# A graph attention layer on one Trainium2 core: batches of eight tiles, with Q and E laid out by feature

## The chip, the cores and the metric

The kernel runs on one core of a Trainium2 chip. Its time is the device time of one execution in microseconds (us). Engines are called TensorE (PE; PEld is its weight load), VectorE (DVE), ScalarE (ACT), GpSimd (POOL) and SyncE (SP); "ACTq", "SPq" and so on are the sequencers that feed them. SBUF is the on-chip memory, PSUM the memory that TensorE writes.

## What is computed

There are N = 6250 nodes with 128 features and E = 206,250 edges, sorted by destination, each with 128 features. With eight heads of sixteen features:

```python
Qh = (h @ WQ).reshape(N, H, D); Kh = (h @ WK).reshape(N, H, D); Vh = (h @ WV).reshape(N, H, D)
Eh = (edge_attr @ WE).reshape(-1, H, D)
score = jnp.einsum('ehd,ehd,ehd->eh', Kh[src], Qh[dst], Eh) * inv_sqrt_d
score = jnp.exp(jnp.clip(score, -5.0, 5.0))
msg = Vh[src] * score[:, :, None]
wV = jax.ops.segment_sum(msg, dst, num_segments=N)
Z = jax.ops.segment_sum(score, dst, num_segments=N)
h_out = wV / (Z[:, :, None] + 1e-06)
x = _layernorm(x + h_out)
```

## The kernel before

**Tiles and batches.** The edges are cut into 1612 tiles of 128; `cut_batches` (L62) makes batches of B = 4 tiles, the last eight tiles in smaller ones. At the start K and V of all nodes go as rows of 1 KB into a table `kv` in memory (`table`, L256), while the first twelve batches gather rows of x and project them themselves (`project`, L408).

**K and V of an edge.** For each tile `gather` (L388) issues one indirect DMA from GpSimd (L397), which brings the 128 rows of K and V of the tile's source nodes. The first gather of a batch waits by hand (L401 to L405) for TensorE's expansion `qps` of a batch some way back: `lag` (L343) is 12 batches at first and falls by one every 40 batches to 3. The other gathers of the batch wait for nothing else that is written out. Buffers: GB = 14 batches.

**Column tiles.** Some tiles, one at the end of two batches in five from batch 32 on, are not gathered (L392). Their 128 columns of x are copied one by one out of the transposed x, which stays in SBUF, with four bytes per partition and an address from a register: 96 on ScalarE in 12 runs of 8, 32 on VectorE in 4 runs of 8 (`columns`, L352; COLA, COLV). Each run is preceded by one load of its addresses into registers (L365, on the sequencer), the copies are L370. TensorE then projects the tile (`project_columns`, L379), VectorE puts it in place (L386). 146 tiles are built so.

**Q of an edge.** Q's rows of a window of 42 nodes are held in three bfloat16 parts (126 rows, `qw`). A one-hot of the destinations, turned so that edges are on the free axis (`onehotT`, `stage_0t`, L450), expands them: in `stage_a` each tile's 128 columns of `onehotT` are the weights and `qw` is streamed (L464). E's product takes each tile's edge features as weights and streams `we` (L469). Both results have edges on partitions.

**Scores and messages.** `stage_b` on VectorE: K times Q (L475), times E (L478), sum per head (L481), clip (L484). `weigh` on ScalarE: the exponent into PSUM (L490) and into the message tile (L492). `messages` on VectorE: V times the exponent (L519). `stage_c` on TensorE: a one-hot of destinations within a window of 64 (`stage_0`, L437, two batches in one operation) times the messages, summed in PSUM over eight tiles (L541); ScalarE copies two such sums at once (L552). `finish` (L507) puts windows together, `layernorm` (L735) follows step by step through `fill`.

**Order of the work.** From batch 12 on the order of instructions on every engine is the order in which the program writes them. The loop (L585) writes for step b: loads on SP, expansion and E product of batch b, gathers of batch b+2, the first half of ScalarE's column copies, the score steps of batch b−1 with one-hots of batch b+2 and small steps between them, the messages of batch b−2, VectorE's column copies, the exponents of batch b−1, ScalarE's other half of columns, and the sums of batch b−2.

Of the kernel before, what the change touches and what calls it, by code (L numbers as in the profile page):

```python
# [20 lines left out]
B = 4  # L21
# [8 lines left out]
GB = 14  # L30
XB = 12
LOCK = XB + 6
STEP = 3
GLEAD = 2
OHB = 5
# [5 lines left out]
AHEAD = 2  # L41
EB = 6
SLAG = 2
# [8 lines left out]
COL0 = 32  # L52
COLP = (5, 2)
COLA = (8, 12)
COLV = (8, 4)
COLL = 8
RING = 4096
SUMS = 8
# [4 lines left out]
def cut_batches():  # L63
    out, t = [], 0
    while t < NT:
        k = B
        if t >= NT - TAIL:
            k = 2 if NT - t > 3 else 1
        out.append(range(t, t + k))
        t += k  # L70
    return out
# [30 lines left out]
def edge_attention(ctx: ExitStack, tc: tile.TileContext, x, xT, srcT, srcC, dstT, dstB, dst0, bnd, lo, eaT,  # L102
# [26 lines left out]
    onehots = [cp.tile([P, HW + 2 * B * P], F32, name=f"onehot{i}") for i in range(OHB)]  # L129
# [11 lines left out]
    with ExitStack() as fast:  # L141
# [80 lines left out]
        def count_inside():  # L222
# [7 lines left out]
            pc = psT.tile([1, 1], F32, name="pc", tag="oT")  # L230
# [9 lines left out]
        psT = fast.enter_context(tc.tile_pool(name="psT", bufs=2, space=bass.MemoryType.PSUM))  # L240
        psA = fast.enter_context(tc.tile_pool(name="psA", bufs=2, space=bass.MemoryType.PSUM))
        psX = fast.enter_context(tc.tile_pool(name="psX", bufs=1, space=bass.MemoryType.PSUM))

        iota_p = psX.tile([P, HW], F32, name="iota_p")
        exp_p = psX.tile([P, B, H], F32, name="exp_p")
        nc.vector.tensor_copy(iota_p, iota_f[:, :HW])

        def pair_bank(i, name, shape):

            pool, tag = ((psE, "eps"), (psT, "oT"), (psQ, "qps"), (psT, "oT"))[i % 4]  # L250
            return pool.tile(shape, F32, name=name, tag=tag)
# [32 lines left out]
        def q_rows(q):  # L284
            n = min(P, N - q * P)
            ps = psT.tile([P, D], F32, name="qrows", tag="oT")
# [56 lines left out]
        def lag(b):  # L343

            return max(STEP, 12 - (b - LOCK) // 40)

        col_tiles, xT_bytes = {}, xT_sb.bitcast(U8)
        used = [0]
# [23 lines left out]
        def project_columns(b):  # L372

            if b not in col_batches:
                return
            g = gathered[b]
            k = col_batches.index(b)
            pk = psT.tile([P, 2 * D], F32, name="colkv", tag="oT")
            nc.tensor.matmul(pk, col_tiles.pop(k), wkv_sb, start=True, stop=True)  # L379
            projected.append((g, pk))  # L380
# [27 lines left out]
        def project(g, n):  # L408

            pt = psT.tile([P, B, P], F32, name="xtps", tag="oT")  # L410
            for i in range(n):
                nc.tensor.transpose(pt[:, i, :], g[:, i, :D], ident)
            xgT = wp.tile([P, B, P], F32, name="xgT", tag="kq", bufs=2)
            nc.scalar.copy(xgT[:, :n], pt[:, :n])
            for i in range(0, n, 2):
                k = min(2, n - i)
                pk = pair_bank(i // 2, "kvps", [P, 2, 2 * D])
                for j in range(k):
                    nc.tensor.matmul(pk[:, j, :], xgT[:, i + j, :], wkv_sb, start=True, stop=True)  # L419
                nc.scalar.copy(g[:, i:i + k, :], pk[:, :k, :])  # L420

        def together(b):

            t0 = batches[b][0]
            n = len(batches[b])
            if n == B and b + 1 < nbat and len(batches[b + 1]) == B and t0 % (2 * B) == 0:
                return [b, b + 1]
            return [] if n == B and t0 % (2 * B) else [b]

        def stage_0(b):  # L430
            group = together(b)
            if not group:
                return
            t0, n = batches[b][0], sum(len(batches[i]) for i in group)
            tl = onehots[used[0] % OHB]
            used[0] += 1
# [3 lines left out]
            for i in group:  # L440
                st8[i] = tl, HW + (batches[i][0] - t0) * P - HW * pair_of(batches[i][0])[1], None

        def stage_0t(b):
            group = together(b)
            if not group:
                return
            t0, n = batches[b][0], sum(len(batches[i]) for i in group)
            ohT = wp.tile([QROWS, 2 * B * P], BF16, name="onehotT", bufs=3)
# [3 lines left out]
            for i in group:  # L452
                tl, at, _ = st8[i]
                k = (batches[i][0] - t0) * P
                st8[i] = (tl, at), ohT[:, k:k + len(batches[i]) * P]

        def stage_a(b, g):
            t0, n = batches[b][0], len(batches[b])
            if b < XB:
                project(g, n)  # L460
            oh, ohT = st8.pop(b)
            pq = psQ.tile([P, B, D], F32, name="qps")
            for i in range(n):
                expanded[b] = nc.tensor.matmul(pq[:, i, :], ohT[:, i * P:i * P + P], loaded[t0 // WT],  # L464
                                               start=True, stop=True)
            pe = psE.tile([P, B, D], F32, name="eps")
            ea = ea_tiles(t0, n)
            for i in range(n):
                nc.tensor.matmul(pe[:, i, :], ea[:, i * P:i * P + P], we_sb, start=True, stop=True)  # L469
            st8[b] = [n, g, oh, pq, pe]  # L470

        def stage_b(b):
            n, g, oh, pq, pe = st8[b]
            t0 = wp.tile([P, B, D], F32, name="kq", bufs=2)
            nc.vector.tensor_tensor(t0[:, :n], g[:, :n, :D], pq[:, :n], op=ALU.mult)  # L475
            yield
            t1 = wp.tile([P, B, D], F32, name="kqe", bufs=2)
            nc.vector.tensor_tensor(t1[:, :n], t0[:, :n], pe[:, :n], op=ALU.mult)  # L478
            yield
            sc = wp.tile([P, B, H], F32, name="sc")  # L480
            nc.vector.tensor_reduce(sc[:, :n], t1[:, :n].rearrange("p b (h d) -> p b h d", h=H),  # L481
# [3 lines left out]
            st8[b] = [n, g, oh, sc]  # L485

        def weigh(b):
# [3 lines left out]
            m = wp.tile([P, B, MW], F32, name="msg")  # L491
# [8 lines left out]
        def add_windows(ps, q, first, stop):  # L500

            parts = windows(q)
            for i, (k, s) in enumerate(parts):
                nc.tensor.matmul(ps, shift[:, P - s:2 * P - s], sums[k // 2][:, k % 2],  # L504
                                 start=first and i == 0, stop=stop and i == len(parts) - 1)

        def finish(j):  # L507

            q = 2 * j
            ps = psT.tile([P, 2, MW], F32, name="finps", tag="oT")  # L510
# [13 lines left out]
        def stage_c(b):  # L524
            n, g, oh, m = st8.pop(b)
            for i in range(n):
# [7 lines left out]
                u = k if final else k // 2  # L534
                first = u not in aggs
                if first:
                    aggs[u] = psA.tile([P, 2, MW], F32, name="agg")
                    if final:
                        add_windows(aggs[u][:, 0], QL, True, False)
                tail = k == NT if t == NT - 1 else pair_of(t + 1)[0] != k  # L540
                nc.tensor.matmul(aggs[u][:, 0 if final else k % 2], oh[0][:, oh[1] + i * P:oh[1] + i * P + P], m[:, i, :],  # L541
                                 start=not final and t % (2 * G) == 0, stop=tail)
                if tail and final:
# [5 lines left out]
                    norms.append(layernorm(nc, sp, aggs.pop(u)[:, :1], xbs.pop(QL), out, QL, 1, stores))  # L549
                elif tail and (k % 2 == 1 or t == LAST - 1):  # L550
                    sums[u] = sp.tile([P, 2, MW], F32, name="sum", bufs=SUMS)
                    nc.scalar.copy(sums[u][:, :k % 2 + 1], aggs.pop(u)[:, :k % 2 + 1])  # L552
                    while len(finished) < QL // 2 and all(v // 2 <= u for v, _ in windows(2 * len(finished) + 1)):
                        ready.append(len(finished))
                        finished.append(u)

        gathered = {b: gather(b) for b in range(2)}
        for b0 in range(0, NB, KB):
# [3 lines left out]
            for b in range(len(gathered), min(XB, nbat)):  # L562
                if (b - 2 if b < 5 else b) * KB > b0:
# [249 lines left out]
```

## Time and profile before

| | |
|---|---|
| median of 3 runs | 2586.32 us (2565.03 to 2592.5) |
| profiled execution | 2567.26 us |
| its span, first to last instruction | 2565.4 us |
| mean granted TensorE clock | 0.75 |
| DMA | 380.81 MB, mean 148 GB/s |
| gathers on GpSimd | 1418 of K and V rows, 48 of x |
| ScalarE column copies | 14016, 189 ns each from start to end |

A row of a group reads: line, engine, operation, output<-input, shapes, count, then busy us and mean ns of one, then the idle time before them and what ended it. A row of stretches reads: stretch in us from the start, its length, busy us and count of each engine asked for, granted clock, DMA share, GB/s. "issue" is time in which an engine waited for nothing that the profile shows. The copies of one run overlap: each lasts 0.19 us from start to end, and they start less than 0.1 us apart.

### The profile page before, as it was taken

Reading aid. Unit: us, or ns where it says so; the run is one execution under the profiler, and the core shown is the slowest. Engines: PE = TensorE matmul, PEld = TensorE weight load, DVE = VectorE, ACT = ScalarE, POOL = GpSimd, SP = SyncE. Lnnn points to the kernel's source line nnn. Section 1 sums busy time; section 2 is a strip of 40 time slices with the busy share of each in tenths; the row PEclk is TensorE's granted clock in tenths of the full one; section 3 lists DMA queues with packets and bytes.
Section 4 is the critical chain, followed back from the end, with each engine's and each line's share of the span. In section 5 each row is a group of like instructions: output and inputs, shape, how many; then the busy total and the mean of one; then the engine's idle time right before and its main releaser. Section 6 shows DMA issues by size and latency. Waiting matters only on the chain.

```text
span 2565.4 us, 49832 instructions
## 1 busy us (share of the span) xinstructions
PE 1624.0 (63%) x9342; PEld 1407.1 (55%) x9342; DVE 1843.5 (72%) x8070; ACT 1644.0 (64%) x15015; POOL 1396.9 (54%) x1473
## 2 busy tenths in 40 slices
PE   5656566676666666666666655667666656566665
PEld 3446555565665555555555555556556555455555
DVE  2436678878777777777767777877877777777786
ACT  1211667777776677676767767777776666776760
POOL 6446555555555455555554555555655555555564
PEclk7777777777776777776777768777876777777787
DMA  7545445645554464455444544564654455545542
GB/s 233 153 130 179 136 125 157 176 134 169 153 148 132 134 176 138 123 147 174 130 135 136 175 140 129 147 175 137 183 147 126 136 144 164 145 131 144 173 145 79
DMA packets 171028, 380.81 MB, mean 148 GB/s; under 512 B 58653, under 2 KB 84569, under 8 KB 170707
## 3 DMA queue, kind: packets, MB, share of 16 engines
q0 software_dynamic: 69584, 189.03, 25.8%
q1 hardware_dynamic: 99983, 187.46, 24.4%
q14 instruction: 244, 2.00, 0.2%
q8 instruction: 77, 1.26, 0.2%
q10 hardware_dynamic: 1140, 1.06, 0.1%
HBM read 362.61 MB, written 14.81 MB: 147 GB/s over the span
## 4 chain that ended last, share of the span: by engine, by line
ACT 46%; issue 25%; DVE 11%; PE 8%; ACTq 6%; another core or an unknown queue 3%; DMA 1%; DVEq 0%; SPq 0%
ACT xcol L370 42%; ACTq L365 6%; DVE xcol L370 2%; PE agg L541 2%; PE eps L469 2%; ACT msg L492 2%; DVE kqe L478 2%; DVE msg L519 1%; DVE kq L475 1%; PE finps L504 1%; ACT exp_p L490 1%; PE kvps L419 1%; DVE sc L481 1%; ACT sum L552 1%
## 5 line engine op out<-in xcount | busy, mean ns | idle before, releaser
L397 POOL DMA_INDIRECT kvrows<-kv,src x1418 | 1350.3, 952 | 1120.4 <-PE qps L464 420.4
L370 ACT COPY xcol<-xT_sb 128x4 uint8 x14016 | 1499.0, 189 | 573.0 <-issue 560.3
L541 PE MATMUL agg<-msg,onehot 128*128 128x136 f32 x3224 | 639.1, 358 | 441.3 <-DVE msg L519 316.8
L541 PEld LDWEIGHTS agg<-msg,onehot 128*128 128x128 f32 x3224 | 562.4, 254 | 492.2 <-ACT msg L492 276.5
L469 PE MATMUL eps<-we_sb,ea 128*128 128x128 f32 x3224 | 599.6, 343 | 164.5 <-DVE kqe L478 95.3
L469 PEld LDWEIGHTS eps<-we_sb,ea 128*128 128x128 f32 x3224 | 517.8, 244 | 220.6 <-DVE kqe L478 128.7
L519 DVE TENSOR_TENSOR msg<-kvrows,exp_p 128x512 f32<-128x512 f32 x406 | 275.9, 679 | 488.8 <-ACT exp_p L490 276.4
L370 DVE COPY xcol<-xT_sb 128x4 uint8 x4672 | 410.9, 192 | 30.2 <-issue 23.0
L464 PE MATMUL qps<-qw,onehotT 126*128 126x128 bf16 x1612 | 193.5, 254 | 240.7 <-DVE kq L475 163.2
L464 PEld LDWEIGHTS <-onehotT 126*128 126x128 bf16 x1612 | 154.7, 117 | 325.3 <-issue 306.8
L478 DVE TENSOR_TENSOR kqe<-kq,eps 128x512 f32<-128x512 f32 x406 | 274.6, 676 | 52.3 <-remote 30.7
L475 DVE TENSOR_TENSOR kq<-kvrows,qps 128x512 f32<-128x512 f32 x406 | 273.7, 674 | 37.5 <-remote 21.3
L481 DVE TENSOR_REDUCE sc<-kqe 128x32 f32<-128x512 f32 x406 | 272.8, 672 | 5.8 <-DVE y L761 0.5
L490 ACT ACTIVATE exp_p<-sc 128x32 f32<-128x32 f32 x406 | 78.3, 193 | 139.7 <-DVE sc L484 76.8
L437 DVE TENSOR_TENSOR onehot<-iota_p,dst_sb 128x512 f32<-128x512 f32 (+2 forms) x206 | 137.6, 669 | 11.0 <-remote 9.0
L379 PE MATMUL colkv<-wkv_sb,xcol 128*128 128x256 f32 x292 | 127.9, 533 | 0.0
L504 PE MATMUL finps<-sum,shift 128*128 128x136 f32 x640 | 95.2, 310 | 17.1 <-ACT sum L552 11.1
L504 PEld LDWEIGHTS finps<-sum,shift 128*128 128x128 f32 x640 | 91.1, 219 | 19.6 <-ACT sum L552 13.1
L492 ACT ACTIVATE msg<-sc 128x32 f32<-128x32 f32 x406 | 87.2, 215 | 22.2 <-issue 21.7
L450 DVE TENSOR_SCALAR onehotT<-relb,node 126x1024 bf16<-126x1024 bf16 (+2 forms) x206 | 99.8, 485 | 1.8 <-DMA relb<-relD 1.7
L484 DVE TENSOR_SCALAR sc<-sc 128x32 f32<-128x32 f32 x406 | 83.7, 206 | 4.2 <-issue 3.8
L379 PEld LDWEIGHTS colkv<-wkv_sb,xcol 128*128 128x128 f32 x292 | 69.1, 285 | 0.0
(73 smaller groups left out, 568.9 us busy)
## 6 DMA issues: line engine op xcount, KB each, us to landing
ea<-eaT SPq DMA_DIRECT2D x201, 512.0 KB
relb<-relD SPq DMA_DIRECT2D x100, 504.0 KB
kvrows<-kv,src POOLq DMA_INDIRECT x1418
qw<-qs SPq DMA_DIRECT2D x202, 31.5 KB
kv<-kvst SPq DMA_DIRECT2D x12, 512.0 KB
qs<-qst SPq DMA_DIRECT2D x48, 96.0 KB
xb<-x SPq DMA_DIRECT2D x24, 128.0 KB
out<-h SPq DMA_DIRECT2D x24, 128.0 KB
```

The costliest lines, as they stand in the source:

```text
L365: at = nc.values_load_multi_w_load_instructions(col_at[k % col_half:k % col_half + 1, k // col_half, j:j + size], engines=(engine,), min_v ...
L370: copy(to[:, 4 * (j + c):4 * (j + c) + 4], xT_bytes[:, ds(at[c] - XT_AT, 4)])
L379: nc.tensor.matmul(pk, col_tiles.pop(k), wkv_sb, start=True, stop=True)
L397: ins = nc.gpsimd.indirect_dma_start(out=g[:k, i, :f], out_offset=None, in_=rows, in_offset=bass.IndirectOffsetOnAxis(ap=src_col(t)[:k], a ...
L464: expanded[b] = nc.tensor.matmul(pq[:, i, :], ohT[:, i * P:i * P + P], loaded[t0 // WT], start=True, stop=True)
L469: nc.tensor.matmul(pe[:, i, :], ea[:, i * P:i * P + P], we_sb, start=True, stop=True)
L475: nc.vector.tensor_tensor(t0[:, :n], g[:, :n, :D], pq[:, :n], op=ALU.mult)
L478: nc.vector.tensor_tensor(t1[:, :n], t0[:, :n], pe[:, :n], op=ALU.mult)
L481: nc.vector.tensor_reduce(sc[:, :n], t1[:, :n].rearrange("p b (h d) -> p b h d", h=H), axis=AX.X, op=ALU.add)
L504: nc.tensor.matmul(ps, shift[:, P - s:2 * P - s], sums[k // 2][:, k % 2], start=first and i == 0, stop=stop and i == len(parts) - 1)
L519: nc.vector.tensor_tensor(m[:, :n, :D].rearrange("p b (h d) -> p b h d", h=H), g[:, :n, D:].rearrange("p b (h d) -> p b h d", h=H), exp_p[ ...
L541: nc.tensor.matmul(aggs[u][:, 0 if final else k % 2], oh[0][:, oh[1] + i * P:oh[1] + i * P + P], m[:, i, :], start=not final and t % (2 * ...
```

## The change

A batch is eight tiles (B = 8), and one iteration of the loop handles eight. E and Q are made with features on partitions: `qw` and `we` are the weights, and 512 edges at a time are streamed. ScalarE copies Q out of PSUM into `eq`, VectorE multiplies it in place by E's product (`product`), TensorE turns the result with eight transposes into PSUM (`turn`), and VectorE multiplies that by K. The score has one multiplication by K (1024 elements wide) and one with E per eight tiles. The expansion of batch b+1 is written in iteration b, after the transposes of batch b. PSUM holds Q, E and the turned product in two banks each, one buffer each; sums, exponents and the small users share the last two banks.

Constants go with it: GB 8, XB 6, one batch of gathers written ahead, a lag of 6 batches that falls by one every 20 to 2. ScalarE's part of a column tile is 6 runs of 16 copies (COLA), and three batches in four have a column tile. The built program has 12,960 column copies on ScalarE, which is 135 tiles (the description says 133), with 810 loads. Window sums are copied one by one.

```diff
-B = 4
+B = 8
-GB = 14
-XB = 12
-LOCK = XB + 6
-STEP = 3
-GLEAD = 2
-OHB = 5
+GB = 8
+XB = 6
+LOCK = XB + 3
+STEP = 2
+GLEAD = 1
+OHB = 3
-EB = 6
-SLAG = 2
+EB = 5
+SLAG = 1
-COL0 = 32
-COLP = (5, 2)
-COLA = (8, 12)
+COL0 = 16
+COLP = (4, 3)
+COLA = (16, 6)
 COLV = (8, 4)
-COLL = 8
+COLL = 4
...
-            return max(STEP, 12 - (b - LOCK) // 40)
+            return max(STEP, 6 - (b - LOCK) // 20)
...
+            pq = psQ.tile([P, B * P], F32, name="qps")
+            pe = psE.tile([P, B * P], F32, name="eps")
+            for i in range(0, n * P, G * P):
+                j = min(n * P, i + G * P)
+                expanded[b] = nc.tensor.matmul(pq[:, i:j], loaded[t0 // WT], ohT[:, i:j], start=True, stop=True)
+            for i in range(0, n * P, G * P):
+                j = min(n * P, i + G * P)
+                nc.tensor.matmul(pe[:, i:j], we_sb, ea[:, i:j], start=True, stop=True)
+            qT = wp.tile([P, B * P], F32, name="eq", bufs=2)
+            nc.scalar.copy(qT[:, :n * P], pq[:, :n * P])
+            st8[b] = [n, qT, pe]
+
+        def product(b):
+            n, qT, pe = st8[b]
+            nc.vector.tensor_tensor(qT[:, :n * P], qT[:, :n * P], pe[:, :n * P], op=ALU.mult)
+            st8[b] = [n, qT]
+
+        def turn(b):
+            n, eq = st8[b]
+            pp = psP.tile([P, B, D], F32, name="pps")
             for i in range(n):
+                nc.tensor.transpose(pp[:, i, :], eq[:, i * P:i * P + P], ident)
+            st8[b] = [n, pp]
+
+        def stage_b(b, g):
+            n, pp = st8[b]
+            t0 = wp.tile([P, B, D], F32, name="kq", bufs=1)
+            nc.vector.tensor_tensor(t0[:, :n], g[:, :n, :D], pp[:, :n], op=ALU.mult)
             yield
...
+            steps = stage_b(b - 1, gathered.pop(b - 1)) if 0 <= b - 1 < nbat else iter(())
+            next(steps, None)
+            if b < nbat:
+                product(b)
+            fill()
+            if b + 1 < nbat:
+                turned_one_hots(b + 1)
+            fill()
+            if b < nbat:
+                turn(b)
+            if b + 1 < nbat:
+                stage_a(b + 1)
+            next(steps, None)
+            fill()
+            if 0 <= b - 2 < nbat:
+                messages(b - 2)
+            fill()
+            next(steps, None)
+            if 0 <= b - 1 < nbat:
+                weigh(b - 1)
+                one_hots(b - 1)
```

The gathers of batch b+1 and the first half of ScalarE's columns are written at the head of iteration b; after the lines above come the small users, VectorE's columns, ScalarE's other half, and the sums of batch b−2.

191 lines of the change are left out of this document (71 added, 120 removed).

## The prediction

> **What bounds the kernel now.** I read, in this order, the page's busy shares and chain of waits, the totals of waits, the register loads' line, and then stretches of ScalarE's column copies cut by where GpSimd's gathers stood.
>
> ```profile
> span 2565.4 us, 49832 instructions
> PE 1624.0 (63%) x9342; PEld 1407.1 (55%) x9342; DVE 1843.5 (72%) x8070; ACT 1644.0 (64%) x15015; POOL 1396.9 (54%) x1473
> ACT 46%; issue 25%; DVE 11%; PE 8%; ACTq 6%; another core or an unknown queue 3%; DMA 1%; DVEq 0%; SPq 0%
> ACT xcol L370 <- issue: 560.3, 1033, 1.2
> DVE msg L519 <- ACT exp_p L490: 276.4, 151, 6.1
> ACT exp_p L490 <- DVE sc L484: 76.8, 22, 18.7
> L365 ACTq TENSOR_LOAD <-col_at x1752: 535/555/1799, 251.8 to 2489.9; - x195
> L312 SPq TENSOR_LOAD <-starts x13: 686/1158/1179, 83.5 to 2395.8; - x13
> 252.00:2490.00 2238.00, 1681.01 (x7680) 0.75 0.51 148
> 252.00:2490.00 2238.00, 1594.13 (x14844) 0.75 0.51 148
> ```
>
> No engine is busy over 72%, but the chain is ScalarE: 46% its work, 25% "issue", 6% its sequencer's loads. The largest wait is ScalarE's column copies behind "issue", 560 us in 1033 gaps: no semaphore was missing, the next copy simply did not start. VectorE waits 276 us for ScalarE's exponents, ScalarE only 77 us for VectorE's scores. The last two rows are VectorE and ScalarE in the stretch in which columns are copied. The loads' row gives that stretch: 251.8 to 2489.9 us, 2238.1 us. The schedule starts columns in batch 25 and ends them in batch 389, so 365 batches of four tiles, 6.13 us each, **12.26 us per eight tiles**; there are 182.5 such units. ScalarE's busy time is 8.7 us of each (1594.13 / 182.5), the gaps 3.1 us (560.3 / 182.5): together 11.8 of 12.26. ScalarE is the bound there.
>
> When do the gaps come? First GpSimd in a run of seven gathers, then the column copies on ScalarE in the seven slots of 1.25 us from its start, and in one slot after it (columns: length, busy us and count, clock, DMA share, GB/s).
>
> ```profile
> 1209.04 0.94 POOL L397 DMA_INDIRECT kvrows<-kv,src  x1 [1.36 <-PE qps L464]
> 1210.29 0.94 POOL L397 DMA_INDIRECT kvrows<-kv,src  x1 [0.30 <-issue]
> ...
> 1209.04:1210.29 1.25, 1.25 (x15) 1.00 1.05 346
> 1210.29:1211.54 1.25, 1.09 (x12) 1.00 1.05 368
> 1211.54:1212.79 1.25, 0.38 (x3) 1.00 1.06 377
> 1212.79:1214.04 1.25, 0.37 (x3) 1.00 1.08 243
> 1214.04:1215.29 1.25, 0.11 (x1) 0.65 1.01 222
> 1215.29:1216.54 1.25, 0.29 (x2) 0.50 1.02 259
> 1216.54:1217.79 1.25, 0.46 (x3) 0.50 0.95 300
> 1219.00:1220.25 1.25, 1.07 (x11) 0.50 0.37 133
> ```
>
> Beside the first two gathers ScalarE copies at full rate, from the third on it falls to one to three copies a slot, and after the run it recovers. The DMA engines are full from the first slot on, so their load alone is not it. The next rows are sums over all 155 runs of back-to-back gathers between 300 and 1500 us: copies beside the first gather, the second, the third, the fourth (105 runs have one), and everything past 5 us.
>
> ```profile
> sum 193.75, ACT 179.15; mean ACT 1.16
> sum 193.75, ACT 175.93; mean ACT 1.14
> sum 193.54, ACT 129.71; mean ACT 0.84
> sum 130.04, ACT 45.15; mean ACT 0.43
> sum 139.63, ACT 38.71; mean ACT 1.11
> ```
>
> Busy shares 92%, 91%, 67%, 35%, 28%. A lone copy counts 0.19 us and one in a row 0.095 us (below), so I read 11.6, 11.4, 7, 3 and 2.5 copies per 1.25 us. **A long unbroken run of gathers starves ScalarE; a short one does not.** That is what the change touches without naming it.
>
> **The change part by part**, per eight tiles of the column stretch.
>
> ```profile
> 1220.19 2.38 ACT L370 COPY xcol<-xT_sb 128x4 uint8 x24
> 1222.47 0.19 ACT L490 ACTIVATE exp_p<-sc 128x32 f32<-128x32 f32 x1
> 1222.61 0.22 ACT L492 ACTIVATE msg<-sc 128x32 f32<-128x32 f32 x1
> 1222.72 1.42 ACT L370 COPY xcol<-xT_sb 128x4 uint8 x14
> L414 ACT COPY xgT<-xtps 128x512 f32<-128x512 f32 x12 | 7.0, 585 | 40.6 <-remote 20.1 <-PE xtps L412 17.7 <-PE qps L464 2.8
> L514 ACT COPY fin<-finps 128x272 f32<-128x272 f32 x24 | 9.1, 379 | 23.3 <-PE finps L504 12.3 <-PE eps L469 4.3 <-PE qps L464 3.9
> L475 DVE TENSOR_TENSOR kq<-kvrows,qps 128x512 f32<-128x512 f32 x401 | 271.9, 678 | 37.5 <-remote 21.3 <-PE agg L541 6.6 <-ACT kvrows L420 3.9
> L475 DVE TENSOR_TENSOR kq<-kvrows,qps 128x256 f32<-128x256 f32 x3 | 1.2, 413 | 0.0
> 105.03 0.60 PE L412 MATMUL xtps<-ident,kvrows 128*128 128x128 f32 x4
> 120.89 0.27 PE L412 MATMUL xtps<-ident,kvrows 128*128 128x128 f32 x1
> 1201.41 0.68 DVE L475 TENSOR_TENSOR kq<-kvrows,qps 128x512 f32<-128x512 f32 x1
> 1202.01 0.68 DVE L437 TENSOR_TENSOR onehot<-iota_p,dst_sb 128x512 f32<-128x512 f32 x1
> 260.00:2480.00 2220.00, 1421.93 (x8225) 1238.34 (x8224) 1667.07 (x7620) 1582.85 (x14743) 1213.72 (x1277) 0.75 0.51 148
> ```
>
> *Column copies.* The program has 12,960 of them on ScalarE, 135 tiles of 96, where it had 14,016. They run in 180 iterations (13 to 192), 72 each, against 76.8 per eight tiles. A copy costs 0.095 us (24 in 2.38 us, the last 0.19): minus 0.46.
>
> *Exponents.* A pair takes 0.25 us (1222.47 to 1222.72); two pairs become one of twice the width, about 0.31: minus 0.19.
>
> *Q copy, new on ScalarE.* From 272 to 512 elements a copy grows by 206 ns, 0.86 ns an element; 1024 take 1.03 us, 0.94 with the overlap that neighbours have: plus 0.94. It stands bare on the bounding engine. Its bounds are 0.94 and, if it falls in a starved stretch where one instruction takes about half a microsecond anyway, 0.4; I take the first. Queued behind it are the exponents, all column copies, the sums. VectorE's product waits for it, and behind the product the turned one-hots, the score reduction and the messages; PE's transposes and next batch wait for that. ScalarE's own wait for Q is covered: the next expansion follows the product and the transposes some 3 us after this copy, and ScalarE has over 10 us of other work until then. So I add no further wait.
>
> *Sums of the windows.* One copy of 136 elements per eight tiles for one of 272 per sixteen: plus 0.02.
>
> *Register loads.* Sixteen registers per load for eight. Now a load of 0.555 us hides behind the eight copies ahead of it, 0.76 us; the only load of sixteen in the trace is SP's, 1.158 us. Per load the cost lies between 0 (all hidden) and 0.60 (all its growth bare), with 4.5 loads between 0 and 2.7 us. Today's loads, the nearest rows on this engine, are hidden, and a starved stretch hides more: I take 0.3. [...]
>
> *Gathers, the step that decides.* Each batch's first gather waits for TensorE's expansion of an earlier batch, the others for nothing. A gather takes 1.25 us (1209.04 to 1210.29); the 155 runs above hold 850.7 us, 4.4 gathers each. A batch of eight makes them seven or eight, 7.25 on average (8 less 0.75 column tiles), 9.06 us. They start at the expansion two or more batches back, so the rows themselves come in time. Now: 155 × (11.6 + 11.4 + 7) + 105 × 3 + 139.63 / 1.25 × 2.5 = 5244 copies in 850.7 us of runs, 6.16 a microsecond. Then: 11.6 + 11.4 + 7 + 3 + 3.25 × 2.5 = 41.1 in 9.06 us, 4.54. That is 1.62 × 9.06 = 14.7 copies per iteration that must be made outside the run at about 0.1 us: plus 1.5. Bounds: 0 (the starving does not follow the length), and 1.8 if the later gathers starve it like the fifth slot above, one copy.
>
> *TensorE.* Expansion and edge products keep their columns but load weights a quarter as often; eight transposes come at 0.11 us ((0.60 − 0.27) / 3), 0.9 us. TensorE is busy 7.8 us of 12.26 and has room. *VectorE.* 512 elements take 678 ns, 256 take 413, so 1024 about 1.21 us, where two ops of 512 start 0.60 us apart: four wide ops save some 0.3 us, half the clips and 1.6 column copies 0.2 more, of its 9.2 us (1681.01 / 182.5). Nothing on the path; if ScalarE were relieved, VectorE at 8.7 and GpSimd at 9.06 would be next. *SP.* The same loads, one chunk per batch, three ahead; hidden.
>
> Sum: 12.26 − 0.46 − 0.19 + 0.94 + 0.02 + 0.3 + 1.5 = **14.37 us**. Outside the column stretch the kernel now spends 2565.4 − 2238.1 = 327 us on 152 tiles; then it is 172 tiles, the extra 20 at the end, where 52 tiles take 75.5 us (1.45 each): 356 us. Total 356 + 180 × 14.37 = 2943 us, and 1.9 us around the span (2567.26 against 2565.4): **2945 us**. The profiled execution is 0.7% below the median of 2586.32 us, so the median after may be 20 us higher.
>
> **Rivals.**
>
> *Run length does not matter* (the gaps go with the number of gathers): the 1.5 falls away, 12.87 us, 2674 us. Against it: slots one and two are unharmed in 155 runs. For it: past 5 us only 139.63 us were seen.
>
> *Faster: the gaps go with ScalarE's own instructions.* [...] It decides when gaps and Q copy together come out below 3.7 us. For it: copies are 14,000 of ScalarE's 15,000 instructions. Against: the gaps begin with the third gather and end with the run. [...]
>
> *Loads stand bare* (no more than the eight copies that hide a load today stand ahead of one of 1.158 us, so 0.40 is bare each time): 1.8 in place of 0.3, 15.87 us, 3215 us.
>
> *They cancel:* no more than 1% from before.
>
> **How the numbers follow.** Forecast 0.46; run length without effect 0.20; faster 0.17; bare loads 0.12; cancelling 0.05. The likeliest alone lies between 2790 us (Q copy at 0.4, loads hidden) and 3215 us (loads at 1.8); loads with all their growth bare, 2.7, would give 3377 us, and I leave that out as part of the bare loads' 0.12. The range leaves out the faster case and what lies beyond bare loads: 2560 to 3220. The three runs before spread by 1.1%, so about 1% is what can be told from no change: faster 0.17, same 0.05, slower 0.78.
>
> **What would show it.** Right: the gathers in runs of seven or eight; ScalarE's column copies behind "issue" well above 3.1 us per eight tiles (about 4.6); the column stretch near 180 × 14.4 us; VectorE waiting at its new product for the Q copy; Q copy near 1.03 us; ScalarE's load near 1.1 us. Wrong: issue gaps no larger than now beside runs of eight, ScalarE waiting for TensorE or VectorE for more than 1 us per batch, or another engine carrying the chain.

## The result, and the profile after

The kernel after takes 2813.92 us in the median (2806.21 to 2820.44), the kernel before beside it 2581.77 us: a ratio of 1.090, 95% interval 1.084 to 1.097. It is slower, by less than forecast: 131 us below the predicted 2945. The profiled execution took 2814.37 us, with a span of 2812.6 us. In two of the sittings that follow the kernel before itself took 1947 and 1949 us in the median, and not 2554 to 2582; nothing in the kernel explains that, so each run is compared with the before of its own sitting, of kind A (2554 to 2582 us, as the result) or kind B (1947 and 1949 us).

The page of after, its longest waits (us in total, times, longest), and the loads of ScalarE:

```profile
span 2812.6 us, 41664 instructions
PE 1629.9 (58%) x7314; PEld 1229.7 (44%) x7314; DVE 1710.5 (61%) x6703; ACT 1699.2 (60%) x13865; POOL 1405.0 (50%) x1484
```

```profile
ACT xcol L371 <- issue: 599.8, 998, 1.2
...
DVE msg L514 <- ACT sum L544: 485.3, 129, 11.1
PE agg L533 <- ACT agg L485: 475.2, 93, 11.7
```

```profile
L366 ACTq TENSOR_LOAD <-col_at x810: 1005/1042/1781, 267.2 to 2713.5; - x162
```

No engine is busy over 61%, and VectorE, at 72% before, is no nearer to being the bound. The loads again mark the column stretch: 2446.3 us, **13.59 us** for each of the 180 iterations, where before took 12.26 and the forecast was 14.37. The other 366 us stand against a forecast of 356. So 180 × (14.37 − 13.59) = 140 us of the miss lie in the column stretch, and 10 us on the other side outside it.

What ScalarE did in that stretch in after (length, then busy us and count of PE, PEld, DVE, ACT, POOL, clock, DMA share, GB/s), and its groups there (busy and mean ns, then idle time before them):

```profile
267.00:2714.00 2447.00, 1414.04 (x6318) 1068.54 (x6318) 1541.17 (x6373) 1628.21 (x13680) 1218.74 (x1285) 0.77 0.45 134
```

```profile
L371 ACT COPY xcol<-xT_sb 128x4 uint8 x12939 | 1388.6, 190 | 610.8 <-issue 599.8
L455 ACT COPY eq<-qps 128x1024 f32<-128x1024 f32 x180 | 180.4, 1002 | 46.7 <-PE qps L450 45.0 <-issue 1.5
L544 ACT COPY sum<-agg 128x136 f32<-128x136 f32 x180 | 47.1, 262 | 35.2 <-remote 12.3 <-PE eps L453 11.3 <-issue 6.1
L487 ACT ACTIVATE msg<-sc 128x64 f32<-128x64 f32 x180 | 43.8, 243 | 0.9 <-issue 0.9
L485 ACT ACTIVATE agg<-sc 128x64 f32<-128x64 f32 x180 | 40.0, 222 | 0.2 <-issue 0.2
L509 ACT COPY fin<-bank 128x272 f32<-128x272 f32 x21 | 8.1, 385 | 130.2 <-remote 90.0 <-PE bank L499 24.7 <-PE qps L450 9.0
```

The same groups of before, in its stretch:

```profile
L370 ACT COPY xcol<-xT_sb 128x4 uint8 x14000 | 1497.3, 189 | 572.2 <-issue 559.5 <-DVE kq L475 0.5 <-DVE y L761 0.5
L492 ACT ACTIVATE msg<-sc 128x32 f32<-128x32 f32 x366 | 78.7, 215 | 22.2 <-issue 21.7 <-PE qrows L287 0.3
L490 ACT ACTIVATE exp_p<-sc 128x32 f32<-128x32 f32 x365 | 70.1, 192 | 27.6 <-issue 20.5 <-DVE sc L484 5.6 <-DVE w L759 1.3
L552 ACT COPY sum<-agg 128x272 f32<-128x272 f32 x91 | 34.1, 375 | 3.6 <-issue 2.4 <-remote 0.6 <-PE agg L541 0.5
L514 ACT COPY fin<-finps 128x272 f32<-128x272 f32 x22 | 8.3, 378 | 18.4 <-PE finps L504 7.4 <-PE eps L469 4.3 <-PE qps L464 3.9
```

Divide both by their iterations (180, and 182.5 units of eight tiles). ScalarE's work went from 1594.13 / 182.5 = 8.74 to 1628.21 / 180 = 9.05 us, plus 0.31. The gaps before column copies went from 3.07 to 3.33 us, plus 0.27. Its idle time before the Q copy, the sum and fin is 212.1 us, 1.18 an iteration; before had 71.8 us, 0.39, at the last four rows: plus 0.79. Together that is 1.37, and the stretch grew by 1.33. The forecast had 0.31 of work, 1.8 of gaps (1.5 beside gathers, 0.3 at loads), and no waits.

The same idle time can be split by what ended it, since part of it before other instructions than column copies is "issue" too. By the rows above "issue" is 604.1 us in before and 608.5 in after, 3.31 and 3.38 us an iteration: plus 0.07. All else, ScalarE waiting for another engine or for something that the profile does not name, is the rest of 644.0 us (2238.1 − 1594.1) and 818.1 us (2446.3 − 1628.2): 0.22 and 1.16, plus 0.95. So ScalarE starves hardly more than before, and what is new is waits.

Where the gaps lie now: ScalarE beside one run of gathers in after, by gather slots of 1.25 us (length, ACT busy and count, clock, DMA share, GB/s), then instruction by instruction:

```profile
1132.30:1133.55 1.25, 1.25 (x14) 0.79 0.00 0
...
1136.05:1137.30 1.25, 1.25 (x6) 0.50 0.34 105
1137.30:1138.55 1.25, 0.99 (x10) 0.50 0.38 105
1138.55:1139.80 1.25, 0.29 (x2) 0.50 0.38 105
1139.80:1141.05 1.25, 0.36 (x3) 0.50 0.39 105
```

```profile
1136.23 1.00 ACT L455 COPY eq<-qps 128x1024 f32<-128x1024 f32 x1
1137.14 0.22 ACT L485 ACTIVATE agg<-sc 128x64 f32<-128x64 f32 x1
1137.30 0.24 ACT L487 ACTIVATE msg<-sc 128x64 f32<-128x64 f32 x1
1137.44 0.85 ACT L371 COPY xcol<-xT_sb 128x4 uint8 x8
1139.41 0.29 ACT L371 COPY xcol<-xT_sb 128x4 uint8 x2 [1.13 <-issue]
```

ScalarE starves as before, but in this run from the sixth gather, not the third; the Q copy and the exponents went through undisturbed in the fourth and fifth slots (from 1136.05 us on). The DMA engines are at 38% here, so full DMA engines aren't needed for it.

### The profile page after: what moved, and what is told of

It reads as the page before. It is cut to its first block, busy times and chain, and to the rows that moved or that the text cites. A ratio compares the mean times of both kernels' runs of the same rounds, so it can differ in the third digit from the quotient of the medians.

```text
span 2812.6 us, 41664 instructions
## 1 busy us (share of the span) xinstructions
PE 1629.9 (58%) x7314; PEld 1229.7 (44%) x7314; DVE 1710.5 (61%) x6703; ACT 1699.2 (60%) x13865; POOL 1405.0 (50%) x1484
## 5 line engine op out<-in xcount | busy, mean ns | idle before, releaser
L371 ACT COPY xcol<-xT_sb 128x4 uint8 x12960 | 1390.7, 190 | 610.8 <-issue 599.8
L514 DVE TENSOR_TENSOR msg<-kvrows,agg 128x1024 f32<-128x1024 f32 (+2 forms) x206 | 246.2, 1195 | 562.2 <-ACT sum L544 485.3
L467 PE MATMUL pps<-ident,eq 128*128 128x128 f32 x1612 | 273.6, 325 | 294.5 <-DVE eq L460 219.1
L453 PE MATMUL eps<-ea,we_sb 128*128 128x512 f32 (+1 forms) x812 | 430.6, 655 | 0.3 <-issue 0.3
L467 PEld LDWEIGHTS pps<-ident,eq 128*128 128x128 f32 x1612 | 231.1, 171 | 343.4 <-issue 259.9
L473 DVE TENSOR_TENSOR kq<-kvrows,pps 128x1024 f32<-128x1024 f32 (+2 forms) x206 | 245.8, 1193 | 37.0 <-DMA kvrows<-kv,src 17.6
L460 DVE TENSOR_TENSOR eq<-eq,eps 128x1024 f32<-128x1024 f32 (+2 forms) x206 | 245.4, 1191 | 31.7 <-ACT eq L455 14.0
L455 ACT COPY eq<-qps 128x1024 f32<-128x1024 f32 (+2 forms) x206 | 202.9, 985 | 96.8 <-PE qps L450 72.8
L476 DVE TENSOR_REDUCE sc<-kq 128x64 f32<-128x1024 f32 (+2 forms) x206 | 243.7, 1183 | 19.9 <-DVE onehotT L436 17.4
L453 PEld LDWEIGHTS eps<-ea,we_sb 128*128 128x128 f32 x812 | 177.1, 219 | 159.1 <-issue 118.4
L450 PE MATMUL qps<-onehotT,qw 126*128 126x512 bf16 x406 | 145.2, 443 | 1.2 <-PE pps L467 0.5
```

What stands on the lines that cost most here:

```text
L371: copy(to[:, 4 * (j + c):4 * (j + c) + 4], xT_bytes[:, ds(at[c] - XT_AT, 4)])
L450: expanded[b] = nc.tensor.matmul(pq[:, i:j], loaded[t0 // WT], ohT[:, i:j], start=True, stop=True)
L453: nc.tensor.matmul(pe[:, i:j], we_sb, ea[:, i:j], start=True, stop=True)
L455: nc.scalar.copy(qT[:, :n * P], pq[:, :n * P])
L460: nc.vector.tensor_tensor(qT[:, :n * P], qT[:, :n * P], pe[:, :n * P], op=ALU.mult)
L467: nc.tensor.transpose(pp[:, i, :], eq[:, i * P:i * P + P], ident)
```

## The experiments

### Is it the waits through shared PSUM? (kind A, before 2580.54 us)

In after the exponents lie in one PSUM tile with the window sums, and `finish` stands behind `place_columns` in one bank. So VectorE's messages wait for ScalarE's sum copy of the iteration ahead (485 us above), TensorE's sums for the exponents (475 us), and the copy of fin for VectorE's placing (143.7 us of idle time before 24 copies in the whole kernel). Theory W says that these are what makes the kernel slower. Rival S says that ScalarE is held by the start of its copies, and time freed elsewhere comes back as gaps.

**a_exp_sbuf**: the messages' exponents in SBUF.

```diff
-            nc.scalar.activation(exp_p[:, :n], sc[:, :n], AF.Exp, scale=0.25)
+            ex = wp.tile([P, B, H], F32, name="ex", bufs=2)
+            nc.scalar.activation(ex[:, :n], sc[:, :n], AF.Exp, scale=0.25)
...
-                exp_p[:, :n, :, None].to_broadcast([P, n, H, DH]), op=ALU.mult)
+                ex[:, :n, :, None].to_broadcast([P, n, H, DH]), op=ALU.mult)
```

> The kernel after, with the exponents that the messages use in an SBUF tile of two buffers in place of the PSUM tile that they share with the window sums. Theory W (the new cost is waits that come from this shared tile): VectorE's messages no longer wait for ScalarE's sum copy, TensorE's sums no longer for the exponents, and ScalarE's idle time before the sum copy (121.8 us) and the Q copy (96.8 us) shrinks by more than half; 100 to 200 us less than 2814, so 2610 to 2720 us. Rival S (ScalarE is held by the issue of its column copies, and time freed elsewhere comes back as gaps before the next copies): the two waits shrink, the gaps before column copies grow beyond 600 us by as much, 2780 to 2840 us.

2864.59 us, 1.109 of before (1.101 to 1.117), 25 us above what S allowed. Two waits and the messages' group of this kernel:

```profile
ACT xcol L371 <- issue: 696.7, 1190, 1.9
...
DVE eq L460 <- ACT eq L455: 208.3, 32, 10.9
```

```profile
L515 DVE TENSOR_TENSOR msg<-kvrows,ex 128x1024 f32<-128x1024 f32 (+2 forms) x206 | 245.5, 1192 | 5.3 <-ACT xgT L417 4.5 <-ACT ex L486 0.5 <-issue 0.3
```

The wait at the messages is gone: 5.3 us of idle time there. ScalarE's gaps grew by 97 us, VectorE now waits at its product for the Q copy, 208 us, and the kernel is no faster. W falls for this wait: taking it away did not help. It was a place where VectorE met a late ScalarE.

**a_fin_early**: `finish` at the head of the iteration. It overwrites a projected column tile that waits in the same bank in the 24 iterations concerned, so part of the output is not the reference's; the work is the same.

```diff
+            for j in ready:
+                finish(j)
+            ready.clear()
             norms.extend(waiting)
...
             place_columns()
-            for j in ready:
-                finish(j)
-            ready.clear()
```

> The kernel after, with the node rows' finish written at the head of an iteration, ahead of the score steps, in place of behind the placing of the column tile. Theory W: ScalarE's wait at the copy of fin (143.7 us in 24 copies, 6 us each) goes, because TensorE's window sums no longer stand behind VectorE's placing in the shared bank; about 100 us less than 2814, 2690 to 2740 us. Rival S: the wait moves to the next instruction or comes back as gaps before column copies, 2790 to 2840 us.

2803.03 us, 1.084 of before (1.077 to 1.092). Its groups:

```profile
L371 ACT COPY xcol<-xT_sb 128x4 uint8 x12960 | 1400.7, 190 | 679.6 <-issue 670.2
...
L509 ACT COPY fin<-bank 128x272 f32<-128x272 f32 x24 | 9.0, 377 | 9.4 <-PE bank L499 9.4
```

The wait for fin fell from 143.7 us over the whole kernel to 9.4, the gaps rose from 599.8 to 670.2, and the time moved by 11 us, less than after's own two measurements differ (1.090 above, 1.081 in after_again below). Rival S fits both: ScalarE's idle time in the whole span, span less busy time, is 1113 us in after (2812.6 − 1699.2; 1074 in after_again), 1119 in a_exp_sbuf (2840.4 − 1721.4) and 1091 in a_fin_early (2799.5 − 1708.3). It changes its label, hardly its size.

### Does the length of a run of gathers matter? (same sitting)

**b_long_runs**: before, with only every second batch's first gather made to wait.

```diff
-                if i == 0 and b >= LOCK:
+                if i == 0 and b >= LOCK and b % 2 == 0:
```

> The kernel before, with only every second batch's first gather made to wait, so that two batches of four are gathered in one run of seven or eight, as in the kernel after. Theory L (the prediction's term of 1.5 us per eight tiles): the gaps before column copies grow from 560 us by about 270, and the time to about 2830 us. Rival N: gaps 540 to 600 us and 2560 to 2600 us.

2876.78 us, 1.113 of before (1.106 to 1.121), with one wait of ScalarE:

```profile
ACT xcol L370 <- issue: 798.2, 1340, 1.3
```

Theory L, the prediction's: the gaps grew by 238 us, 1.30 us per eight tiles where 1.5 was forecast, and the kernel by 296 us; the 58 us beyond the gaps are not explained. In the order of before, run length is worth about what the prediction said.

In after it is worth less. ScalarE's busy time in the slots of the first to the seventh gather, summed over the 82 to 87 runs of seven or eight between 300 and 1500 us; first b_long_runs, then after:

```profile
sum 108.75, ACT 107.06; mean ACT 1.23
sum 108.75, ACT 105.82; mean ACT 1.22
sum 108.75, ACT 84.58; mean ACT 0.97
sum 106.25, ACT 35.19; mean ACT 0.41
sum 102.50, ACT 34.63; mean ACT 0.42
sum 102.50, ACT 31.09; mean ACT 0.38
sum 102.50, ACT 22.84; mean ACT 0.28
```

```profile
sum 103.75, ACT 99.61; mean ACT 1.20
sum 103.75, ACT 97.19; mean ACT 1.17
sum 103.75, ACT 92.26; mean ACT 1.11
sum 103.75, ACT 75.25; mean ACT 0.91
sum 103.75, ACT 52.40; mean ACT 0.63
sum 103.75, ACT 36.98; mean ACT 0.45
sum 103.57, ACT 23.92; mean ACT 0.29
```

The means add to 4.91 us of busy time in a run for b_long_runs and 5.76 for after. The difference, 0.85 us, is near the Q copy's 1.00. ScalarE's instructions in each run up to its first gap over 0.35 us, its sequencer's loads included, counted from the traces between 300 and 2400 us, are 35 in the median in before, 37 in b_long_runs, 36 in a_exp_sbuf and 44 in after (middle half 34 to 53), while the time until then is 3.4, 3.7, 3.8 and 5.2 us. That suggests theory C: a run lets some 30 instructions start and then about two a microsecond (the prediction's 3 copies per 1.25 us beside the fourth gather of before, 2.5 past 5 us), and a long one uses up one of them.

The traces can be asked further, by where the Q copy falls in a run of seven or eight gathers in the column stretch; here the loads are not counted. In a_exp_sbuf 90 runs have no Q copy in their first 5 us: the first large gap comes after 3.7 us and 33 instructions in the median, as in b_long_runs (3.7 us, 33). In 49 runs the Q copy starts in the first 2.5 us: 4.6 us and 34 instructions. The copy puts the starving off by nearly its own length and counts as one instruction, which is what theory C says of it. In after, too, the 31 runs without a Q copy starve from 3.7 us on, and the 56 with one in the first 2.5 us from 4.9 us. But its 46 runs with a Q copy between 3.7 and 5 us go undisturbed past 3.7 us before that copy starts, and starve only from 6.1 us on, after 50 instructions; ahead of them ScalarE had stood idle for 2.4 of 4 us, against 0.9 ahead of the 56. So the stock is not fixed, and something besides the copy is at work in after; that idle time ahead of a run enlarges the stock is a guess from these figures. These are comparisons within a trace, not experiments.

**a_short_runs**: after, with the fifth gather of a batch waiting for window sums of an earlier batch.

```diff
-                if i == 0 and made is not None:
+                if i == G and b >= LOCK:
+                    made = summed[b - lag(b) - 3]
+                if i in (0, G) and made is not None:
...
-                nc.tensor.matmul(agg[:, u % 2], oh[:, i * P + HW - HW * half:][:, :P], m[:, i, :],
+                summed[b] = nc.tensor.matmul(agg[:, u % 2], oh[:, i * P + HW - HW * half:][:, :P], m[:, i, :],
```

> The kernel after, with the fifth gather of each batch made to wait for the window sums of an earlier batch, half an iteration later, so that gathers come in runs of at most four. Theory L (the prediction's: a gather late in a long unbroken run starves ScalarE): the gaps before column copies fall from 600 us towards 300, and the time by 150 to 270 us, 2540 to 2660 us. Rival N (the length of a run does not matter; the gaps go with the number of gathers or with what else runs): gaps 570 to 630 us, 2790 to 2850 us, or more if rows now come late.

2861.49 us, 1.108 of before (1.101 to 1.116); gaps 592.4 us, hardly fewer than in after. GpSimd's largest wait is the added one:

```profile
POOL kvrows L398 <- PE agg L535: 646.6, 125, 8.6
```

It mostly moved the runs and did not cut them: the first gather's own wait was then often over (235.2 us, 51 times), and the second half of a batch is gathered in one run with the first half of the next. Of 237 runs in this trace, 143 still have seven or eight gathers, and only 85 have four or fewer.

The short ones do starve ScalarE less. From the start of a run to the start of the next, its idle time behind "issue" is 0.41 us in the mean for runs of three gathers (30 of them between 300 and 2600 us), 1.14 for four (45), 3.80 for seven (92) and 5.06 for eight (34). So in this order of work, too, gaps go with run length. Yet nothing was won: a run of three and one of four together take 14.1 us, one of seven 13.9 us, and ScalarE's other idle time is 2.41 us beside the two and 0.77 beside the one. Idle time changed its label again. What holds such an iteration at 14 us is not known; the added wait itself can be part of it.

### The terms by themselves (kind B, before 1948.98 us)

These four met a ScalarE that is little starved: in their order, 22, 155, 181 and 112 us of gaps before column copies.

**a_load8** and **a_q_dve**, two terms of the sum undone in after:

```diff
-COLA = (16, 6)
+COLA = (8, 12)
```

```diff
-            nc.scalar.copy(qT[:, :n * P], pq[:, :n * P])
+            nc.vector.tensor_copy(qT[:, :n * P], pq[:, :n * P])
```

> The kernel after, with ScalarE's column copies in twelve runs of eight behind loads of eight registers, as before, in place of six runs of sixteen. The prediction's term (0.3 us per iteration for loads of sixteen): 50 us less, 2760 us. [...] Theory C: twice as many loads add to ScalarE's instructions, but hide behind the copies: 2790 to 2850 us.

> The kernel after, with Q copied out of PSUM by VectorE in place of ScalarE. The prediction's step (0.94 us bare on the bounding engine): 180 times 0.94 less, about 2645 us. Theory C (while the Q copy runs, ScalarE uses up one instruction only, so that its microsecond mostly replaces gaps): ScalarE's gaps grow by 100 us or more, and the time stays within 2770 to 2860 us. Theory W: VectorE, which already waits 485 us for ScalarE's sums, gets a ninth microsecond of work in the chain of an iteration: 2814 to 3000 us.

a_load8: 1963.32 us, 1.009 of before (1.006 to 1.011). Some of its waits:

```profile
POOL kvrows L398 <- issue: 397.0, 1303, 0.3
...
ACT eq L455 <- PE qps L450: 121.3, 61, 17.3
...
POOL kvrows L398 <- PE qps L450: 68.5, 30, 12.6
ACT fin L509 <- PE bank L499: 55.9, 23, 5.0
ACT sum L544 <- PE agg L533: 40.5, 22, 3.8
...
ACT xcol L371 <- issue: 22.1, 78, 1.5
```

The gaps are 22 us, where after in kind A had 600, and the waits before the Q copy, the sum and fin shrank with them. VectorE's wait at the messages for ScalarE's sum, with the same shared PSUM tile, is 40 us in place of 485: the shared tile costs little where ScalarE keeps up. GpSimd waits for TensorE only 68.5 us; it issues one gather behind the other. This kernel, which differs from after in the loads alone, is within 1.1% of before here. What the load size costs in a sitting of kind A this run can't say.

a_q_dve: 2498.79 us, 1.282 of before (1.279 to 1.286), with two waits that bear on it:

```profile
ACT agg L485 <- DVE sc L479: 589.4, 192, 15.6
...
DVE eq L455 <- PE qps L450: 402.1, 205, 9.1
```

VectorE now stands at the Q copy until TensorE has turned the product that VectorE itself has just made and expanded the next batch, 402 us; everything behind it, the scores above all, is late, and ScalarE waits 589 us for them. On ScalarE the copy's wait is mostly hidden by column copies (46.7 us in after's stretch), as the prediction said; on VectorE it is not. The three theories, made for a before of 2580 us, had it at 1.03, 1.07 to 1.11 and 1.09 to 1.16 of it: all too fast.

**a_half_cols** (after with `COLP = (5, 2)`, 0.4 column tiles per eight tiles) and **b_half_cols** (before with `COLP = (5, 1)`, the same share):

> The kernel after, with 0.4 column tiles per batch of eight in place of 0.75, the others gathered. Theory C (ScalarE can start about 30 instructions from the beginning of a run of gathers and then about 2 a microsecond until it ends; the first large gap stands behind 35, 37 and 44 ScalarE instructions of a run in before, b_long_runs and after): an iteration then issues some 47 ScalarE instructions against 48 that a run of 9.5 us lets through, so the gaps before column copies fall from 600 us below 200, and the iteration to 11 or 12 us: 2350 to 2550 us. Rival W (the iteration is set by the waits through the shared PSUM tile, of which ScalarE's copies fill a part): the gaps fall as well, the waits grow in their place, 2700 to 2830 us. Rival L (gaps go with gathers): gaps as now or more, 2750 us or more.

> The kernel before, with one column tile in five batches of four in place of two, the others gathered. Theory C: 45 ScalarE instructions per eight tiles in two runs of gathers that let 40 through each: the gaps before column copies fall from 560 us below 100, and eight tiles come to the 10 us that 7.6 gathers of 1.25 us and the runs' pauses need: 2150 to 2300 us. Rival L (gaps go with the number and the length of the runs of gathers): gaps 500 us or more, and the longer runs take back what the copies save, 2500 to 2650 us.

2001.69 us, 1.027 of before (1.025 to 1.030), and 1973.58 us, 1.013 (1.010 to 1.016). With little starving to remove, fewer copies did not make the kernels faster; that the extra gathers cost the 1 to 3% is likely and was not tested. In a_half_cols GpSimd hardly pauses: grouped by pauses over 0.7 us, one run has 1435 gathers, yet little starving goes with it. (Its 181 us of gaps are in 256 pieces; it has 432 loads of 1.04 us, and ScalarE, busy 52%, has fewer copies to make beside them; that the gaps stand at loads was not tested.) So run length alone does not starve ScalarE.

### The kernel after again, and a Q copy by itself

**after_again**: the kernel after, unchanged (kind A, before 2554.25 us).

> The kernel after, unchanged. The kernel before took 2580 us in the runs beside a_exp_sbuf and 1949 us in the runs beside a_load8, whose gaps before column copies are 22 us: ScalarE was held up beside gathers on the one chip and not on the other. Where before takes about 2580 us, the theory that the chip sets the gaps expects 2780 to 2840 us and 570 to 630 us of gaps. Where before takes about 1950 us, it expects gaps below 150 us; then GpSimd sets the pace (1477 gathers at 1.25 us, 1846 us, and some 110 us around them), and the kernel after comes within 1940 to 2000 us, level with before. The rival, that what made after slower are its own waits (362 us before the sum, the Q copy and fin), expects 1.05 or more of before on that chip as well, 2050 us or more.

2768.81 us, 1.081 of before (1.077 to 1.086), with 551.5 us of gaps: the result repeats, a little below the expected figures. The theory that the chip sets the gaps falls with the next sitting: the same chip met kind B eight minutes later, and the sitting of a_load8, on another chip, had met kind B too. What after itself does in kind B stays unmeasured; a_load8 is the nearest.

**b_long_copy**, **b_half_cols_2** and **a_half_cols_2** met kind B, before 1947.19 us. The first is b_long_runs with a stand-in for the Q copy (its edit to the gathers is left out here):

```diff
                 stage_a(b, g)
+                if b % 2 == 0 and b >= LOCK:
+                    spare = wp.tile([P, 1024], F32, name="spare", bufs=1)
+                    nc.scalar.copy(spare, xT_sb[:, LEFT:LEFT + 1024])
```

> The kernel of b_long_runs (1.113 of before, 798 us of gaps before column copies) with one more ScalarE copy of 128x1024 per eight tiles, about 1 us, written behind the edge products of every second batch and used by nobody, as a stand-in for the Q copy; it adds to the output nothing. The prediction's price (0.94 us bare on the bounding engine): 190 times 0.94, 180 us more, 1.18 of before. Theory C (ScalarE can start about 30 instructions from the beginning of a run of gathers and then about 2 a microsecond until it ends; a long instruction uses up one of them): most of the microsecond replaces gaps, these fall by 100 us or more, and the time is 1.10 to 1.14 of before. On a chip on which ScalarE isn't held up beside gathers (before about 1950 us): both expect no effect of the run length, and at most 1.06 of before.

> The kernel before with one column tile in five batches of four in place of two, as b_half_cols, which ran on a chip without these gaps. On a chip with them (before about 2570 us), theory C: 45 ScalarE instructions per eight tiles, in two runs of gathers that let about 40 through each; gaps before column copies fall from 560 us below 100, and the time to 2100 to 2300 us. Rival L (gaps go with the number and the length of the runs of gathers): gaps 400 us or more, and 2400 to 2650 us.

> The kernel after with 0.4 column tiles per batch of eight in place of 0.75, as a_half_cols, which ran on a chip without these gaps. On a chip with them, theory C: 47 ScalarE instructions per iteration against 48 that one run of 9.5 us lets through: the gaps before column copies fall from 600 us below 150, ScalarE's waits before the Q copy, the sum and fin no longer follow from a late ScalarE, and the time is 2050 to 2300 us, within 4% of b_half_cols_2. Rival W (the waits through the shared PSUM tile are after's own): 8% or more above b_half_cols_2.

b_long_copy: 1963.78 us, 1.008 of before (1.007 to 1.010). Two groups and the column stretch of this kernel:

```profile
L370 ACT COPY xcol<-xT_sb 128x4 uint8 x14016 | 1399.3, 192 | 23.4 <-issue 18.2
...
L611 ACT COPY spare<-xT_sb 128x1024 f32<-128x1024 f32 x194 | 202.5, 1044 | 0.0
```

```profile
200.00:1890.00 1690.00, 1221.41 (x8184) 1064.14 (x8184) 1622.91 (x7583) 1635.77 (x14879) 1220.33 (x1281) 0.88 0.66 195
```

Long runs and 202 us of added copies together cost 17 us. ScalarE is busy 1635.77 of 1690 us, 97%, beside as many gathers as in b_long_runs. The other two repeat their first figures: 1973.52 us, 1.013 (1.012 to 1.015), and 2002.23 us, 1.028 (1.026 to 1.030). Theory C's count was therefore not tried by an experiment where it would matter: it rests on the comparisons within the traces above. No kernel here was faster than the before beside it; in kind A the halved columns are untried.

## Why the prediction was right in sign and 131 us too high

The way and, within 5%, the time came out as forecast. Part of that is luck: starving that was forecast hardly came, waits that were not forecast did, and the two errors have opposite signs.

*Right, to the size.* ScalarE's work: forecast plus 0.31 us (−0.46 −0.19 +0.94 +0.02), measured plus 0.31. The Q copy took 1.00 us, forecast 1.03; a load of sixteen registers 1.04, forecast near 1.1. Gathers come in runs of seven or eight. The time outside the columns: 366 us for 356.

*The step that failed: "plus 1.5", the starving beside the longer runs, set down in full beside a bare Q copy.* The prediction had named an overlap of the two as the lower bound of the Q copy, 0.4, and did not take it. Gaps before column copies grew by 0.27 us an iteration, and all idle time behind "issue" by 0.07, for 1.5 beside gathers and 0.3 at loads. The run length is no wrong mechanism: b_long_runs shows 1.30 us of it when the copies stand as in before. The prediction counted copies per slot as if only column copies could stand there. In after the Q copy and the exponents stand in the run's middle, take 1.3 us, and go through undisturbed; the first large gap comes 5.2 us into a run in the median, not 3.7 as in b_long_runs. So the two terms overlap: in a run ScalarE is 0.85 us busier than in b_long_runs. That the long copy itself puts off the starving is borne out within traces (3.7 us without it, 4.6 with it early in a run, in a_exp_sbuf), though by no experiment, as b_long_copy met no starving. It is not all: many runs of after go undisturbed longer than the copy explains, and why is open.

*The second failed step: "So I add no further wait".* ScalarE's idle time before the Q copy, the sum and fin grew by 0.79 us an iteration, and all its waits that are not "issue" by 0.95, against none. At 1.16 us a batch these waits meet one of the prediction's own signs of being wrong, more than 1 us, if those with no engine named are counted; and VectorE's wait at its product for the Q copy, a sign of being right, is 14 us in all. This part of the forecast missed that the exponents share a tile with the sums and that `finish` stands behind the placing. But a_fin_early and a_exp_sbuf took such waits away and came to 11 us less, within what repeats differ by, and 51 us more: with ScalarE starved they trade places with gaps. What holds is the sum, idle time of ScalarE: (2238.1 − 1594.1) / 182.5 = 3.53 us before, (2446.3 − 1628.2) / 180 = 4.55 after. It grew by 1.02 where the forecast had 1.8.

*Loads.* Plus 0.3 was forecast. Gaps at loads and beside gathers stand in one row, which grew by 0.27 in all. If only eight copies, 0.76 us, stood ahead of each load, as the rival of bare loads has it, the loads alone would cost an estimated 1.8, or 1.3 with the load as measured (4.5 × (1.04 − 0.76)). The trace of after disagrees: when most of the loads start, nine or ten copies have still to run, and the first copy behind such a load starts 0.19 us in the median after the instruction ahead of it, some 0.09 us later than the 0.095 of copies in a row.

*Rivals.* "Run length does not matter" gave 2674 us; it is refuted for before's order by b_long_runs, and its time is 140 us too low, so by the time alone it is about as near as the forecast. "Faster" was half right about one thing, that the Q copy does not come on top of the gaps: within a_exp_sbuf a run with the copy early starves from 4.6 us on, one without it from 3.7. But gaps and Q copy came to 3.33 + 1.00 us an iteration, where this rival needed less than 3.7. In kind B, of which the profile before showed nothing, the change with loads of eight is about level: 1.009 for a_load8.

*What stays open.* What makes ScalarE starve in kind A and not in kind B. Between after in kind A and a_load8 in kind B the time of a column copy (190 and 193 ns), the gathers (1429 of K and V rows in each, of 951 and 955 ns) and the DMA bytes of the column stretch (134 GB/s over 2447 us and 198 over 1664, 328 and 329 MB) are the same; the granted clock differs (0.77 and 0.91 in that stretch). It is not the clock of the moment: in the 1.25 us from the start of the fourth to the eighth gather of a run, ScalarE of before is busy 34% where the granted clock is full (140 such slots between 300 and 2400 us) and 32% where it is half (182 slots), and in a_load8 93% at full clock (75 slots). What else goes with a lower mean clock, no run tells.

## What to carry to other kernels

Two costs that fall into the same stretch of one engine are not added: ask which of them would be waiting anyway (in a run of after ScalarE was 0.85 us busier than in one of b_long_runs, near the Q copy's 1.00). A wait in the list is a place where two engines meet, not yet a cause; take it away, and see whether the engine's total idle time falls or only changes its label (1113 us in after, 1119 in a_exp_sbuf, 1091 in a_fin_early). And run the kernel before beside every experiment, since the condition that sets the bound can go away between sittings (2554.25 and 1947.19 us for the kernel before on one chip).

## What the runs showed of the hardware that was not expected

- The same kernel before ran at 2580.54 and at 1948.98 us in two sittings, and on one chip at 2554.25 and 1947.19 us eight minutes apart; the distance is about that of ScalarE's gaps (560 us in before, kind A; 18 and 22 us in b_long_copy and a_load8, kind B).
- In kind A ScalarE's short copies starve while GpSimd issues gathers one behind another, at a DMA share of 0.38 as at 1.0, while copies of 1.00 us pass freely (1.5 us of "issue" before all 180 Q copies of after). Within one trace, a_exp_sbuf, a run with such a copy in its first 2.5 us starves from 4.6 us on, one without from 3.7 us on, behind 34 and 33 instructions.
- Taking sixteen registers in one load costs 1.04 us on ScalarE's sequencer (after, 810 loads), eight 0.56 us (before, 1752): about 60 ns a register, and some 0.07 us besides.
